# Input projections of a GRU scan moved between the start and the end of the scan

## The chip, the cores and the metric

The kernel runs on one NeuronCore of a Trainium2 chip. The metric is the device time of one execution in microseconds; the median of three runs of the kernel before is 1308.48 us (1308.43 to 1308.65). The core has a matrix engine (TensorE, PE), three engines for elementwise work (VectorE or DVE, ScalarE or ACT, GpSimd or POOL) and a queue engine (SyncE, SP) that only issues DMAs. Each engine executes its own list of instructions in order and waits on semaphores for the others.

## The reference

A GRU scans 256 time steps for 16 sequences of width 512. Its outputs pass through a mixture of eight low-rank experts, the best two per token, and the result is added to x. All data are float32.

```python
def cell(h, x):
    gi = x @ W_ih + b_ih            # 512 x 1536
    gh = h @ W_hh + b_hh            # 512 x 1536
    r = sigmoid(i_r + h_r)
    z = sigmoid(i_z + h_z)
    n = tanh(i_n + r * h_n)
    return (1 - z) * n + z * h

hs = scan(cell, cond, x over time)
logits = hs / norm(hs) @ router_w
top-2 of softmax(logits), renormalised -> combine
out = x + sum over e of combine[e] * (hs @ Wa[e] @ Wb[e])
```

gh of a step needs the step before; gi needs only x, and can be computed at any earlier moment.

## The kernel before, in words

**Layout.** 16 sequences fill only 16 rows of a matmul's stationary operand, so the kernel puts the four quarters of the 512 columns side by side on the array: every product is made in four column strips of 32, and a block of W (128 x 1536) is split along the contraction into four quarters q. A "pair" m is two consecutive time steps (2m and 2m+1) held together in 32 rows; there are 128 pairs, and four pairs (eight steps) make a block of x of which there are 32 (`NB`). The input side of a pair is `gate_in(m, q)` for q = 0 to 3 (L274): four matmuls of 256 columns for the gates r and n (L281), four of 128 columns for z (L289), accumulated in PSUM on top of a start value that ScalarE copies there, `seed(m)` (L255, L261). x must first be turned by VectorE, `trans_x(m)` (L266, L269).

**A step.** `step` (L903) multiplies the turned state with W_hh: r and n for all q (L914), then z (L924). ScalarE applies tanh for r (L940), for z (L945) and for n (L949); VectorE does the elementwise work between (L947 to L956) and turns the new state (L959) for the next step's matmuls, and back (L967). TensorE waits for L959 unless other matmuls fill the time. In the program, behind the recurrent matmuls of a step, stand half of `gate_in` for the next pair and then the pieces that a planner picks.

**The start.** SP issues, in this order: x of block 0 (`load_x`, L127: 8 DMAs of 32 KB), W_ih and W_hh (`load_w`, L152: 16 DMAs of 192 KB each, four per quarter q), x of block 1, the weights of router and experts (`wr_sb`, `wa_sb`, `wb_sb`, the last one DMA of 2 MB). `gate_in` for pair 0 and three quarters of pair 1 are computed as W_ih arrives. In step 0, `arrive(q)` scales a quarter of W_hh when it has come (L987 on VectorE, L988 on ScalarE), and behind it, for q = 1 to 3, eight matmuls of 512 columns on zeros (L993) are issued whose result nobody reads. The last quarter of pair 1 stands behind step 0's recurrent matmuls.

**The mixture.** 29 of the 32 blocks go a sparse way in four chunks of 7, 11, 7 and 4 blocks (`CHUNKS`). When a chunk is ranked, its tokens are scattered by expert (GpSimd, L551) into slots in DRAM; 86 slabs of 128 slots are then loaded (L652), multiplied by Wa (L691) and Wb (L706) and stored (L715), and gathered again for their tokens (`Combine`, L743, L757). A slab has four matmul pieces of 0.43 us by the planner's costs. Slabs of a chunk begin at the steps in `ready`: 73, 165, 217 and 246. The last three blocks are computed densely (`Moe`).

**The planner.** The whole order is written out when the program is built. Work besides the recurrence is cut into pieces with a cost on TensorE, a least distance in steps from the piece before (`gap`) and places that they take and give (`ROOM`). After each step `choose(spare)` picks pieces in order of rank: routes first, then slabs, combines, dense blocks and last the early pairs (rank 20). Pieces fit while their cost in this step is at most `spare`, which is 0.5, or 1.8 where the next pair needs no `gate_in` (`m + 1 in EARLY`); slabs and dense blocks have due times and can go beyond it on a credit that grows with how much is left.

**Early pairs.** For the pairs in `EARLY`, 82, 86, ... 126, twelve in all, the input side is computed in advance by an agent (`Early`, L359): load x of the pair (8 DMAs of 8 KB, L371), turn it (VectorE, L378), four pieces for r and n (L387), four for z (L392), `keep` (L397: ScalarE copies out of PSUM, GpSimd adds the bias), `store` to DRAM (L408), and `back` (L411, L413) loads it again from step 2m-16 on, for `seed(m)` to copy it into PSUM in place of the bias in step 2m-3. At most two agents work at once (`"early": 2`); they begin before step 2.

Of the kernel before, what the change touches and what calls it, by code (L numbers as in the profile page):

```python
# [8 lines left out]
FP = mybir.dt.float32  # L9
# [12 lines left out]
P = 128  # L22
# [3 lines left out]

EARLY = list(range(82, 128, 4))

# [16 lines left out]
def gru_moe_kernel(  # L45
# [11 lines left out]
    out: bass.AP,  # L57
):


# [33 lines left out]
    B, T, D = x.shape  # L94
    E, _, R = wa.shape
# [30 lines left out]

    def load_x(i):  # L127
        xt = xp.tile([P, NM, P], FP, tag="x", name=f"x_{i}")
        for j in range(NJ):
            for s in range(2):  # L130
                p0 = 32 * j + 16 * s
                sp.dma_start(
                    xt[p0 : p0 + B],
                    x[:, i * TS + s : (i + 1) * TS : 2, j * P : (j + 1) * P],
                )
        xs[i] = xt
# [23 lines left out]

    wih = load_w("wih", w_ih)
    whh = load_w("whh", w_hh)
    load_x(1)
# [91 lines left out]
    def seed(m):  # L255

        if m < T // 2:
            src = early.pop(m) if m in EARLY else bias
            for n, b in enumerate((src[:, 0:3, :], src[:, 3:4, :])):
                b = b.rearrange("p g d -> p (g d)")  # L260
                ins = act.copy(banks[m % 2][n][:, 0 : b.shape[1]], b).ins  # L261
                if seeds:
                    tc.add_manual_dep(ins, seeds[-1].name, SYNC, reason="seen")
                seeds.append(ins)

    def trans_x(m):  # L266
        if m < T // 2 and m not in EARLY:
            xt = xtp.tile([P, NQ, 32], FP, tag="xT", name=f"xT_{m}")
            dve.transpose(  # L269
                xt.rearrange("p q c -> p (q c)"), xs[m // NM][:, m % NM, :]  # L270
            )
            xts[m] = xt

    def gate_in(m, q, seen=None):  # L274

        if m in EARLY:
            return
# [81 lines left out]
    class Early:  # L359
# [5 lines left out]
        def load(self):  # L365
            m = self.m
            self.x = slb.tile([P, D], FP, tag="yg1", bufs=2, name=f"xe_{m}")
            for j in range(NJ):
                for s in range(2):
                    p0 = 32 * j + 16 * s  # L370
                    sp.dma_start(  # L371
                        self.x[p0 : p0 + B, 0:P],
                        x[:, 2 * m + s, j * P : (j + 1) * P],
                    )

        def turn(self):
            self.xt = slb.tile([P, NQ, 32], FP, tag="at", bufs=2, name=f"xTe_{self.m}")
            dve.transpose(self.xt.rearrange("p q c -> p (q c)"), self.x[:, 0:P])  # L378

# [17 lines left out]
        def keep(self):  # L397
            gi = slb.tile([P, 4, P], FP, tag="yg0", bufs=2, name=f"ge_{self.m}")
            act.copy(gi[:, 0, :], self.ps[:, 0, :])
            act.copy(gi[:, 2:4, :], self.ps[:, 2:4, :])  # L400
            pool.tensor_copy(gi[:, 1, :], bias[:, 1, :])
            pool.tensor_add(gi[:, 0, :], gi[:, 0, :], bias[:, 0, :])
            pool.tensor_add(gi[:, 2:4, :], gi[:, 2:4, :], bias[:, 2:4, :])
            self.gi = gi

        def store(self):
            self.dram = dramc.tile([P, 4, P], FP, name=f"gd_{self.m}")
            sp.dma_start(self.dram, self.gi)  # L408
            at_step(2 * self.m - 16, self.back)

# [4 lines left out]
        def plan(self):  # L415
# [8 lines left out]
            pieces[2].gap, pieces[2].takes = 1, ["ps"]  # L424
            pieces[9].then, pieces[9].gives = [("keep",)], ["ps", "at"]
            return pieces

# [551 lines left out]
    seed(1)  # L979
    for m, q in [(0, q) for q in range(NQ)] + [(1, q) for q in range(NQ - 1)]:  # L980
        gate_in(m, q)

    def arrive(q):


        cut = 2 * D
        dve.tensor_scalar_mul(whh[:, q, 0:cut], whh[:, q, 0:cut], 0.5)  # L987
        act.mul(whh[:, q, cut:G], whh[:, q, cut:G], 0.5)  # L988
        if q:
            idle = big(f"idle_{q}")  # L990
            for _ in range(2):
                for j in range(NJ):
                    pe.matmul(  # L993
                        idle[32 * j : 32 * j + 32, :], lhsT=zero[:, 0:32], rhs=zero,
                        start=True, stop=True,
                    )


# [7 lines left out]
    def at_step(n, make):  # L1006
        starts.setdefault(n, []).append(make)
# [98 lines left out]
    for i in range(NB):  # L1106
        rows, rows_next = rows_next, None
        for t in range(TS):
# [82 lines left out]
```

## Time and profile before

| | value |
|---|---|
| median of three runs | 1308.48 us (1308.43 to 1308.65) |
| the profiled execution, its own time | 1301.67 us |
| its span, first to last instruction | 1299.9 us |
| mean granted TensorE clock | 0.992 |
| W_hh's last quarter is scaled at | 35.8 us |
| step 1 begins at | 39.57 us |
| last turn of the state (L959) begins at | 1218.9 us |
| TensorE busy | 1252.2 us (96%) |

A line of the groups or of the timeline gives start and duration in us, engine, source line, operation, output tile, inputs, and in brackets how long the engine stood idle before and what ended that. Lines of waits give in total who waited for whom, how often, and the longest. A line of windows gives a stretch of time, then the busy time of PE, PEld (weight loads), DVE, ACT and POOL with their numbers of instructions, the granted share of TensorE's clock, the share of the 16 DMA engines that was busy, and GB/s.

### The profile page before, as it was taken

To read this page: it belongs to the slowest core of one execution; us is meant where nothing else is said; L and a number is where in the kernel's file an instruction comes from. 1 tells how busy PE (TensorE), PEld (TensorE's weight loads), DVE (VectorE), ACT (ScalarE), POOL (GpSimd) and SP (SyncE) were. 2 spreads that over 40 slices of the span, in tenths; PEclk is the share of its full clock that TensorE was granted. 3 is DMA by queue.
4 is the path that set the end of the run, shared out by engine and by line. 5 is a ranking of instruction groups with operands and counts; after the bars stand their busy time and mean duration, and the time that the engine had idled before them with its cause. 6 is when DMAs were issued, how large, how long until landed. Compare 5 with 4: busy or idle time off the path is not lost. (4 is left out here: it accounts for less than half of the span.)

```text
span 1299.9 us, 68450 instructions
## 1 busy us (share of the span) xinstructions
PE 1252.2 (96%) x30378; PEld 888.0 (68%) x30378; DVE 734.4 (56%) x2678; ACT 391.4 (30%) x1354; POOL 285.4 (22%) x504
## 2 busy tenths in 40 slices
PE   6799999999999999999999999999999999999996
PEld 2477777777777777777777766777777777777652
DVE  1445555555555555555556646666556556676643
ACT  1222232222223333233232323333333333333320
POOL 2000000000421100000100433232114234373552
PEclk7999999999999999999999999999999999999999
DMA  8522322321522221112111544655335446774786
GB/s 196 158 98 86 103 91 80 104 92 47 191 77 62 60 61 54 49 44 60 43 56 57 193 153 122 173 163 150 97 98 184 150 134 183 207 224 144 206 256 179
DMA packets 149477, 158.67 MB, mean 122 GB/s; under 512 B 22646, under 2 KB 103606, under 8 KB 149180
## 3 DMA queue, kind: packets, MB, share of 16 engines
q1 hardware_dynamic: 139760, 123.83, 32.2%
q0 software_dynamic: 9280, 30.42, 7.5%
q8 instruction: 238, 3.90, 1.3%
q14 instruction: 59, 0.48, 0.1%
q10 hardware_dynamic: 140, 0.05, 0.0%
HBM read 84.21 MB, written 69.99 MB: 119 GB/s over the span
## 5 line engine op out<-in xcount | busy, mean ns | idle before, releaser
L914 PE MATMUL rn<-whh,hist 128*32 128x256 f32 x8160 | 493.6, 382 | 19.4 <-DVE hist L959 16.5
L914 PEld LDWEIGHTS rn<-whh,hist 128*32 128x32 f32 x8160 | 247.7, 110 | 201.4 <-DVE hist L959 51.8
L281 PE MATMUL rn<-wih,xT 128*32 128x256 f32 x3712 | 287.9, 381 | 11.3 <-DMA wih<-in_L_cond_W_ih_dram 9.4
L947 DVE SCALAR_TENSOR_TENSOR n<-r,rn 128x128 f32<-128x128 f32 x256 | 73.2, 286 | 362.2 <-ACT r L940 361.2
L924 PE MATMUL z<-whh,hist 128*32 128x128 f32 x8160 | 271.0, 273 | 0.0
L924 PEld LDWEIGHTS z<-whh,hist 128*32 128x32 f32 x8160 | 235.5, 110 | 42.9 <-issue 0.4
L940 ACT ACTIVATE r<-rn 128x128 f32<-128x128 f32 x256 | 70.9, 277 | 426.4 <-PE rn L914 426.4
L289 PE MATMUL z<-wih,xT 128*32 128x128 f32 x3712 | 188.4, 274 | 0.0
L289 PEld LDWEIGHTS z<-wih,xT 128*32 128x32 f32 x3712 | 122.0, 111 | 80.4 <-issue 1.8
L281 PEld LDWEIGHTS rn<-wih,xT 128*32 128x32 f32 x3712 | 112.0, 110 | 12.9 <-DMA wih<-in_L_cond_W_ih_dram 5.1
L945 ACT ACTIVATE z<-z 128x128 f32<-128x128 f32 x256 | 71.0, 278 | 151.1 <-PE z L924 150.5
L952 DVE SCALAR_TENSOR_TENSOR zh<-z,h 128x128 f32<-128x128 f32 x255 | 77.7, 305 | 65.6 <-ACT z L945 65.4
L622 POOL TENSOR_TENSOR nrm<-ss,half 128x1 f32<-128x1 f32 x29 | 16.2, 560 | 411.5 <-ACT ht L620 392.4
L691 PE MATMUL at_ps<-xgT,wag 128*32 128x128 f32 x2752 | 96.8, 273 | 2.2 <-POOL nrm L808 1.4
L706 PE MATMUL y_ps<-wbg,at 128*32 128x256 f32 x1376 | 94.6, 380 | 0.8 <-ACT at L698 0.8
L691 PEld LDWEIGHTS at_ps<-xgT,wag 128*32 128x32 f32 x2752 | 79.1, 110 | 9.8 <-issue 3.1
L959 DVE STREAM_TRANSPOSE hist<-rows 128x128 f32<-128x128 f32 x256 | 79.8, 312 | 8.7
L967 DVE STREAM_TRANSPOSE h<-hist 128x128 f32<-128x128 f32 x256 | 79.7, 311 | 8.7
L956 DVE SCALAR_TENSOR_TENSOR rows<-zh,m 128x128 f32<-128x128 f32 x256 | 76.0, 297 | 8.9
L674 POOL COPY wbg<-wb_sb 128x512 f32 x86 | 55.4, 644 | 114.9 <-PE y_ps L706 114.9
L949 ACT ACTIVATE n<-n 128x128 f32<-128x128 f32 x256 | 77.3, 302 | 7.6 <-DVE n L948 7.3
L714 ACT COPY y<-y_ps 128x512 f32<-128x512 f32 x86 | 50.1, 583 | 94.9 <-PE y_ps L706 85.7
(136 smaller groups left out, 1050.4 us busy)
## 6 DMA issues: line engine op xcount, KB each, us to landing
xg<-x_slots SPq DMA_DIRECT2D x344, 64.0 KB
y_slots<-y SPq DMA_DIRECT2D x86, 256.0 KB
ht<-H SPq DMA_DIRECT2D x58, 256.0 KB
x_slots<-zero SPq DMA_DIRECT2D x50, 256.0 KB
x<-in_x_dram SPq DMA_DIRECT2D x256, 32.0 KB
xr<-in_x_dram SPq DMA_DIRECT2D x32, 256.0 KB
out_dram<-xr SPq DMA_DIRECT2D x32, 256.0 KB
H<-rows SPq DMA_DIRECT2D x232, 32.0 KB
```

What stands on the lines that cost most here:

```text
L281: pe.matmul(rn[32 * j : 32 * j + 32, 0 : 3 * P].rearrange("p (g d) -> p g d", g=3)[:, 0:3:2, :], lhsT=xts[m][:, q, :], rhs=w[:, 0:3:2, j, ...
L289: ins = pe.matmul(zb[32 * j : 32 * j + 32, 0:P], lhsT=xts[m][:, q, :], rhs=w[:, 1, j, :], start=False, stop=(q == NQ - 1), skip_group_chec ...
L691: pe.matmul(self.ps[c32, 0:P], lhsT=self.wa[:, q, c32], rhs=self.xt[:, q, :], start=(q == 0), stop=(q == NQ - 1),)
L706: pe.matmul(self.ps[c32, half], lhsT=self.at[:, c32], rhs=self.wb[:, half], start=True, stop=True,)
L914: pe.matmul(rn[32 * j : 32 * j + 32, 0 : 2 * P].rearrange("p (g d) -> p g d", g=2), lhsT=hT[:, q, :], rhs=w(q, j)[:, 0:3:2, :], start=Fals ...
L924: pe.matmul(zb[32 * j : 32 * j + 32, 0:P], lhsT=hT[:, q, :], rhs=w(q, j)[:, 1, :], start=False, stop=(q == NQ - 1), skip_group_check=True,)
L947: dve.scalar_tensor_tensor(n, r, 1.0, rn[:, P : 2 * P], ALU.add, ALU.mult)
L949: act.activation(n, n, AF.Tanh)
L952: dve.scalar_tensor_tensor(zh, z, 1.0, hrow, ALU.add, ALU.mult)
L956: dve.scalar_tensor_tensor(hn, zh, 0.5, m, ALU.mult, ALU.subtract)
L959: dve.transpose(hist[:, t, :, lo : lo + 32], hn.rearrange("p (q c) -> p q c", q=NQ))
L967: dve.transpose(hrow.rearrange("p (q c) -> p q c", q=NQ), hT)
```

## The change

- The input sides of pairs 2 and 3 (`HEAD`) are computed ahead of the scan by the methods of `Early`: pair 2 behind those of pairs 0 and 1, pair 3 in `arrive`, its r and n behind the first quarter of step 0 and its z behind the second. The results stay in SBUF. The last quarter of pair 1 moves ahead of step 0 as well. The matmuls on zeros go.
- x of block 21 (`EARLY[0] // NM`, pairs 84 to 87) is loaded between W_ih and W_hh and not again later.
- `EARLY` is 84 to 87 and then 92, 95, ... 125: sixteen pairs. The first four take x from that block, without loads, and turn in the step in which they begin; the others turn three steps after their load, before two.
- The agents begin before step 0, and `spare` is 1.8 in steps 0 and 1 and before a `HEAD` pair (steps 2 to 5) too.
- Early results are loaded again from step 2m-6 on.

```diff
-EARLY = list(range(82, 128, 4))
+EARLY = [84, 85, 86, 87] + list(range(92, 128, 3))
+HEAD = [2, 3]
...
-    def load_x(i):
-        xt = xp.tile([P, NM, P], FP, tag="x", name=f"x_{i}")
+    def load_x(i, pool=xp, tag="x"):
+        xt = pool.tile([P, NM, P], FP, tag=tag, name=f"x_{i}")
...
     wih = load_w("wih", w_ih)
+    load_x(EARLY[0] // NM, slb, "xg")
     whh = load_w("whh", w_hh)
...
-            src = early.pop(m) if m in EARLY else bias
+            src = early.pop(m) if m in EARLY + HEAD else bias
...
-        if m < T // 2 and m not in EARLY:
+        if m < T // 2 and m not in EARLY + HEAD:
...
-        if m in EARLY:
+        if m in EARLY + HEAD:
             return
...
         def load(self):
             m = self.m
+            if m in EARLY[:4]:
+                return
...
+            if m in HEAD + EARLY[:4]:
+                rows = xs[m // NM][:, m % NM, :]
+            else:
+                rows = self.x[:, 0:P]
+            dve.transpose(self.xt.rearrange("p q c -> p (q c)"), rows)
...
         def keep(self):
-            gi = slb.tile([P, 4, P], FP, tag="yg0", bufs=2, name=f"ge_{self.m}")
+            tag, bufs = ("xg", 4) if self.m in HEAD else ("yg0", 2)
+            gi = slb.tile([P, 4, P], FP, tag=tag, bufs=bufs, name=f"ge_{self.m}")
...
+            if self.m in HEAD:
+                early[self.m] = gi
...
-            at_step(2 * self.m - 16, self.back)
+            at_step(2 * self.m - 6, self.back)
...
+            pieces[1].gap = 0 if self.m in EARLY[:4] else 3
...
-    for m, q in [(0, q) for q in range(NQ)] + [(1, q) for q in range(NQ - 1)]:
-        gate_in(m, q)
+    for m in (0, 1):
+        for q in range(NQ):
+            gate_in(m, q)
+    head = [Early(m) for m in HEAD]
+    for agent in head:
+        agent.turn()
+    for what in ("rn", "z"):
+        for q in range(NQ):
+            head[0].into(what, q)
+    head[0].keep()
...
-        if q:
-            idle = big(f"idle_{q}")
-            for _ in range(2):
-                for j in range(NJ):
-                    pe.matmul(
-                        idle[32 * j : 32 * j + 32, :], lhsT=zero[:, 0:32], rhs=zero,
-                        start=True, stop=True,
-                    )
+        if q == 1:
+            for n in range(NQ):
+                head[1].into("rn", n)
+        elif q == 2:
+            for n in range(NQ):
+                head[1].into("z", n)
+            head[1].keep()
...
-    at_step(2, lambda: [begin(Early(m), 20) for m in EARLY])
+    at_step(0, lambda: [begin(Early(m), 20) for m in EARLY])
...
-            if m == 0:
-                if t == 0:
-                    gate_in(1, NQ - 1, seen)
-            elif m + 1 < T // 2:
+            if 0 < m and m + 1 < T // 2:
...
-            picked = choose(1.8 if m + 1 in EARLY else 0.5)
+            picked = choose(1.8 if m == 0 or m + 1 in EARLY + HEAD else 0.5)
...
-            if t == 3 and i + 2 < NB:
+            if t == 3 and i + 2 < NB and i + 2 not in xs:
                 load_x(i + 2)
```

More of the change, by code (lines that the diff above doesn't have):

```diff
@@ L376, in turn @@
         def turn(self):
-            self.xt = slb.tile([P, NQ, 32], FP, tag="at", bufs=2, name=f"xTe_{self.m}")
-            dve.transpose(self.xt.rearrange("p q c -> p (q c)"), self.x[:, 0:P])
+            m = self.m
+            self.xt = slb.tile([P, NQ, 32], FP, tag="at", bufs=2, name=f"xTe_{m}")
+            if m in HEAD + EARLY[:4]:
[3 more added lines that the diff above has]
+            dve.transpose(self.xt.rearrange("p q c -> p (q c)"), rows)
         def into(self, what, q):
```

## The prediction

> **What bounds the kernel now.** I read the engine shares first, then who waits for whom, then single steps in the timeline, then windows of the start.
>
> ```profile
> PE 1252.2 (96%) x30378; PEld 888.0 (68%) x30378; DVE 734.4 (56%) x2678; ACT 391.4 (30%) x1354; POOL 285.4 (22%) x504
> ...
> PE rn L914 <- DVE hist L959: 16.5, 25, 3.8
> ```
>
> TensorE looks full, but "busy" includes matmuls that only fill a wait. The timeline of single steps (step n counted from 0; it begins at the first L914 row) tells more:
>
> ```profile
> 52.78 1.93 PE L914 MATMUL rn<-whh,hist 128*32 128x256 f32 x32 [0.30 <-DVE hist L959]
> ...
> 57.19 1.93 PE L914 MATMUL rn<-whh,hist 128*32 128x256 f32 x32 [0.30 <-DVE hist L959]
> ...
> 102.44 1.93 PE L914 MATMUL rn<-whh,hist 128*32 128x256 f32 x32
> 104.19 1.06 PE L924 MATMUL z<-whh,hist 128*32 128x128 f32 x32
> 105.06 0.61 PE L281 MATMUL rn<-wih,xT 128*32 128x256 f32 x8
> ...
> 106.36 0.61 PE L387 MATMUL gi<-wih,xTe 128*32 128x256 f32 x8
> 106.85 1.93 PE L914 MATMUL rn<-whh,hist 128*32 128x256 f32 x32
> ```
>
> Step 4 (52.78) has no early work and takes 4.41 us; step 15 (102.44) has one early matmul group of 0.43 us more and takes 4.41 us too. So a step has a floor of 4.40 us, its chain of gates, and room for about 4.34 us of TensorE work: 2.62 recurrent (102.44 to 105.06), 1.30 for the input side of the next pair (105.06 to 106.36), 0.43 of anything else. What exceeds that is paid one for one:
>
> ```profile
> 1082.84 1.91 PE L914 MATMUL rn<-whh,hist 128*32 128x256 f32 x32
> ...
> 1086.73 1.06 PE L691 MATMUL at_ps<-xgT,wag 128*32 128x128 f32 x32
> 1087.61 1.91 PE L914 MATMUL rn<-whh,hist 128*32 128x256 f32 x32
> ```
>
> Here 0.87 us of slab work makes the step 4.77. Listing all step starts, time above 4.405 per step is 5.6 us in steps 1 to 7, 0.7 in 8 to 77, 6.2 in 78 to 161, 22.8 in 162 to 221 and 21.2 from 222 on; after the last step (1218.9) TensorE works off what is left until 1290. So work taken out of late steps is worth its full time, work put into early free room costs nothing.
>
> **What steps 5 and 6 lose.** They begin at 57.19 and 65.51, and step 7 at 71.60: 14.41 us where 8.81 would do.
>
> ```profile
> 63.12 0.31 DVE L378 STREAM_TRANSPOSE xTe<-xe 128x128 f32<-128x128 f32 x1 [4.58 <-DMA xe<-in_x_dram]
> ...
> 65.51 3.02 PE L914 MATMUL rn<-whh,hist 128*32 128x256 f32 x32 [3.78 <-DVE hist L959]
> ```
>
> The transposition of the second early pair's x waits on VectorE, in order, ahead of the gates of step 5; its loads were issued behind the 2 MB of W_b. The pause also halves TensorE's clock (L914 takes 3.02 instead of 1.93).
>
> **The parts, one by one.**
>
> *1. That stall goes: -5.6 us.* The first four early pairs (84 to 87) read block 21 of x, which is there before W_hh. The first pair with loads of its own (92) gets a place only when the third is stored, in step 9, some 30 us after W_b is in, and turns three steps later. If the stall only moves, 0; its whole amount is the other bound.
>
> *2. x of block 21 ahead of W_hh: +2.5 us.* Eight more DMAs on SP move W_hh (16), x of block 1 (8) and the other weights (21) back. 256 KB at the 230 GB/s of the neighbouring windows would be 1.1 us. But the same kind of load after W_hh leaves a hole:
>
> ```profile
> 32.00:33.00 1.00, 0.62 (x8) 0.00 (x0) 0.26 (x1) 0.28 (x1) 0.00 (x0) 1.00 1.09 250
> 33.00:34.00 1.00, 0.46 (x10) 0.37 (x13) 0.43 (x1) 0.35 (x1) 0.00 (x0) 1.00 0.87 163
> 34.00:35.00 1.00, 1.00 (x20) 0.50 (x16) 0.00 (x0) 0.00 (x0) 0.00 (x0) 1.00 0.45 87
> ...
> 37.00:38.00 1.00, 1.00 (x28) 0.52 (x20) 0.40 (x2) 0.50 (x2) 0.00 (x0) 1.00 0.27 60
> 38.00:39.00 1.00, 0.23 (x8) 0.00 (x0) 0.79 (x4) 0.31 (x1) 0.00 (x0) 1.00 0.85 245
> ```
>
> The last column is GB/s. In the trace each SP DMA waits for the semaphore of the one eight before it, so while eight small ones are in flight no large one is queued. The first DMA behind block 1 of x is issued 0.30 us after the last quarter of W_hh is used (36.06 against 35.76). So W_hh's first issue comes at 22.33 (last quarter of W_ih used) + 0.3 = 22.6; W_ih itself took 5.6 us from first issue (5.23) to first use (10.83); hence W_hh's first quarter at 28.2 instead of 25.82: 2.4, taken as 2.5. Bounds 1.1 and 3.5. All of it is on the path: step 0 ends with the last quarter. The other weights that move back have long slack (W_a and W_b are first read in step 77, block 1 of x in step 4).
>
> *3. Pairs 2 and 3 in the head: 0 on the path.* Each is 16 matmuls of each kind, 2.6 us. Pair 1's last part and pair 2 follow the seven groups that now end at 26.6, so TensorE is free at about 29.8. ScalarE's copies of pair 2 (0.27 + 0.38 us) stand ahead of its scaling of W_hh's first quarter, so that scaling slips from 28.3 to 30.4. Pair 3's parts (1.72 and 0.87) go where the filler matmuls were (3 x 1.72, removed) and its copies stand before the last scaling. The last quarter arrives at 35.76 + 2.5 = 38.3; everything ahead of it on TensorE is done near 36.6. The cover is thus about 1.7 us; without it, what exceeds it is paid. GpSimd's three operations per pair (0.29 + 0.46 + 0.73) are read by seeds at the ends of steps 1 and 3. VectorE's two transpositions lie in the wait.
>
> *4. The clock: +2.0 us.* Without filler matmuls TensorE now pauses from 36.6 to 39.0, works 0.65, and pauses again for the gates of step 0 (2.3 us, formerly cut by pair 1's last part).
>
> ```profile
> 10.00:15.00 5.00, 1.61 (x24) 0.96 (x28) 0.00 (x0) 1.27 (x4) 0.00 (x0) 0.66 1.03 225
> 15.00:20.00 5.00, 1.80 (x25) 0.91 (x20) 0.00 (x0) 0.00 (x0) 0.00 (x0) 0.50 1.02 226
> ```
>
> PEclk (last but two) is 0.66 in the first window: full for 1.6 us, half from about 11.6 on. Before that drop stood a pause of only 1.7 us, 0.9 of work and the start of a pause of 2.6. [...] Half clock adds 0.65 to the last quarter's matmuls and about half of the 2.7 us until it recovers inside step 1. Step 6 paid 6.08 - 4.41 = 1.67 for the same. Bounds 0 and 3.
>
> *5. Early work in steps 1 to 5: 0 now, worth it later.* By the planner's rules step 1 takes 1.72 us of pair 84, steps 2 and 3 take 1.74 each, step 4 none (the next pair must turn first), step 5 takes 1.72, then 0.43 to 0.44 a step. Work of 2.62 + 1.74 fits the floor. Pair 87 ends in step 14, so four pairs are done where one and a half were. At the old pace of 6.7 steps a pair, 13 to 14 are done when slabs take the room (step 78), against 11. The other two or three find room in steps 166 to 169, free of input work while the slabs of the second chunk, which start at 165 and need five steps, aren't ready.
>
> *6. 16 late pairs instead of 12: -7.8 us.* Every early pair frees 1.30 us in two steps, and the planner puts up to 1.8 us of slabs there. From step 170 on, where load exceeds room, there were 22 such steps and are now 28: 6 x 1.30. In steps 170 to 222 the second chunk needs 29 x 1.72 = 50 us, and even the new room is some 43, so none should be idle. Bounds: -3.9 (half unused) and -10.4 (four pairs in full).
>
> *7. The reload.* Pairs are read back from step 2m-6 instead of 2m-16, with the seed (ScalarE) in step 2m-3: three steps and 3.2 us, about 16.5 us. Reloads in the trace are issued up to 12.8 us after their step begins (step 212, behind scatters and x) and land 2.3 to 4.8 us later. The worst is at the edge; mostly 5 us remain. Behind a late seed stand tanh and all later gates. 0, with +4 as bound.
>
> *8. Contention.* Two or three late pairs share buffers with the first combines; steps 169 and 172, where one did so, were 0.5 long each. +0.5, bounds 0 and 3.
>
> Sum: -5.6 + 2.5 + 2.0 - 7.8 + 0.5 = -8.4 us against the profiled execution's 1301.67 (span 1299.9 and 1.8 around it), so 1293.3 there. The runs' median lies 6.8 higher; the same difference gives 1308.48 - 8.4 = **1300.1 us**.
>
> **Rivals.**
>
> *Better:* the clock stays up and the load costs its bytes only: -2.0 and -1.4, so 1296.7. [...]
>
> *The freed steps stay half empty*, because slabs aren't loaded in time for eight free steps in a row: 3.9 less, and 1 more of contention, 1305.0. For it: steps 220 and 221 have no slab today; against: the room still falls short of the need.
>
> *The stall only moves:* 5.6 less, 1305.7. Against it: steps 8 to 77 show no such wait.
>
> *Slower: the late reload.* In the seed (L261), if issue plus landing passes 16.5 us. The four pairs whose reload falls behind an x load (85, 101, 113, 125) at 4 us each give 1316. It decides from 8.4 us in total, half a microsecond per pair. For it: three steps instead of thirteen, in the part with 143 to 225 GB/s; against: the landings above.
>
> **How the numbers follow.** Forecast 0.52, better 0.14, half empty 0.14, stall moves 0.05, late reload 0.15. A measurement tells 0.2% (2.6 us) from nothing. Half empty and stall moved lie near that edge (1305.9): 0.10 of their 0.19 counts as faster, the rest as the same; of the late reload 0.01 is the same and 0.14 slower. Faster 0.76, same 0.10, slower 0.14. The likeliest's own range is 1297.5 to 1303.5; with the other cases and the bounds it is 1295.5 to 1308.0, leaving out the reload and a little below.
>
> **What would show it.** Right: steps 5 and 6 at 4.4; W_hh's scalings 2 to 3 us later; half clock near 39 us; step 7 within 1.5 us of 71.6; steps 166 to 173 at 4.4 to 4.5. Wrong: ScalarE waiting for gl; the last quarter's matmuls behind pair 3; a new VectorE wait for xe; steps above 5 us after 170 as before.

## The result

The changed kernel takes 1313.32 us (median of 22 runs, 1307.61 to 1319.53) where the kernel before takes 1308.43 (22 runs beside it, 1304.80 to 1310.59): ratio 1.0052, 95% interval 1.0041 to 1.0063. It is slower by 4.9 us in the medians and by 6.8 (5.4 to 8.2) by the ratio, which is what I use from here on; the forecast was 8 us faster, and its range ended at 1308.0. The profiled execution of the changed kernel took 1310.03 us (span 1308.3, clock 0.988) against 1301.67 (1299.9, 0.992).

One profiled execution lies up to some 4 us on either side of its kernel's median (b_norm3's 6.0 above), and the profile of before lies 6.8 below. So in what follows a stage of a profile counts where several kernels show the same, and prices are taken from the ratios.

**The start went as forecast.** From the timeline of the changed kernel (start, duration, engine, line, operation):

```profile
38.42 0.69 DVE L1010 TENSOR_SCALAR whh<-whh 128x1024 f32<-128x1024 f32 x1 [2.07 <-DMA x<-in_x_dram]
39.22 1.08 PE L930 MATMUL rn<-whh,h0T 128*32 128x256 f32 x8 [1.91 <-DMA x<-in_x_dram]
42.76 3.47 PE L930 MATMUL rn<-whh,hist 128*32 128x256 f32 x32 [2.03 <-DVE hist L975]
...
62.38 1.93 PE L930 MATMUL rn<-whh,hist 128*32 128x256 f32 x32 [1.68 <-DVE hist L975]
62.51 0.27 DVE L390 STREAM_TRANSPOSE xTe<-x 128x128 f32<-128x128 f32 x1
66.78 1.93 PE L930 MATMUL rn<-whh,hist 128*32 128x256 f32 x32
71.19 1.07 PE L930 MATMUL rn<-whh,hist 128*32 128x256 f32 x16
```

The last quarter of W_hh is scaled at 38.42 (35.76 before), its matmuls and those of step 1 run at half clock (1.08 and 3.47 us), steps 5 and 6 take 4.40 and 4.41 us with no wait for xTe, and step 7 begins at 71.19 (71.60 before). Yet the wait that the forecast meant to shrink grew. Who waits for whom, in the changed kernel (us in total, times, longest):

```profile
PE rn L930 <- DVE hist L975: 22.4, 29, 2.0
...
ACT ht L636 <- DMA ht<-H: 15.2, 5, 5.5
ACT y L730 <- DMA y_slots<-y: 14.3, 6, 5.2
```

It was 16.5 us with a longest of 3.8: the one long wait is gone, and many of about one microsecond have come.

**Where the time came from.** I split each step: TensorE's busy time above 4.405 us is called load, and what the step took beyond the larger of 4.405 and that busy time is called wait. Differences to the kernel before, in us, from the profiled executions (b_16, below, has the new list of late pairs and the old start):

| stage | forecast | after | b_16 |
|---|---|---|---|
| up to step 8 | -1.1 | -0.4 | -1.1 |
| steps 8 to 77 | 0 | +2.3 | +0.1 |
| steps 78 to 161 | 0 | +3.1 | +5.1 |
| steps 162 to 169 | +0.5 | +0.2 | -1.8 |
| steps 170 to 254 | -7.8 | -1.1 | -1.2 |
| behind the start of the last step | 0 | +4.3 | +5.9 |
| sum | -8.4 | +8.4 | +7.0 |

In steps 170 to 254 the load fell from 36.3 to 27.9 us, by 8.4, as the forecast had it (7.8). But the wait rose from 3.7 to 11.0. Here is one such step in the timeline, step 182, which begins at 862.82 and lasts 5.18 us. Before, it took 5.42, with 0.58 of load and 0.44 of wait; now it has no load and 0.77 of wait:

```profile
862.82 1.91 PE L930 MATMUL rn<-whh,hist 128*32 128x256 f32 x32
...
864.87 0.61 POOL L686 COPY wag<-wa_sb 128x512 f32 x1 [0.55 <-PE rn L930]
865.11 0.29 DVE L963 SCALAR_TENSOR_TENSOR n<-r,rn 128x128 f32<-128x128 f32 x1 [0.21 <-ACT r L956]
...
865.43 0.29 DVE L964 SCALAR_TENSOR_TENSOR n<-n,rn 128x128 f32<-128x128 f32 x1
865.43 0.60 POOL L690 COPY wbg<-wb_sb 128x512 f32 x1
...
866.12 0.63 POOL L686 COPY wag<-wa_sb 128x512 f32 x1
866.19 0.70 DVE L970 SCALAR_TENSOR_TENSOR m<-z,n 128x128 f32<-128x128 f32 x1
...
866.70 0.67 POOL L690 COPY wbg<-wb_sb 128x512 f32 x1
866.92 0.58 DVE L972 SCALAR_TENSOR_TENSOR rows<-zh,m 128x128 f32<-128x128 f32 x1
...
868.00 0.42 PE L930 MATMUL rn<-whh,hist 128*32 128x256 f32 x4 [1.09 <-DVE hist L975]
```

GpSimd copies a slab's weights (L686, L690) while VectorE does the gates. L970 takes 0.70 us and ends 0.14 after the copy that it met; L972 takes 0.58 and ends 0.13 after the next one. The medians of their 256 are 0.28 and 0.29. TensorE, with less to do than before, stands idle for 1.09 us behind them. In this step VectorE's list shows no wait for GpSimd: the lost time is inside the duration of L970 and L972. It is so in most late steps: of the changed kernel's wait behind step 170, 9.7 of some 11 us stand in the 14 steps in which the gate operations together took at least 0.25 us more than 0.29 apiece.

### The profile page after: what moved, and what is told of

Same layout as the page of the kernel before. It is cut to its first block, busy times and chain, and to the rows that moved or that the text cites. A ratio compares the mean times of both kernels' runs of the same rounds, so it can differ in the third digit from the quotient of the medians.

```text
span 1308.3 us, 68408 instructions
## 1 busy us (share of the span) xinstructions
PE 1247.6 (95%) x30330; PEld 891.8 (68%) x30330; DVE 741.3 (57%) x2678; ACT 394.5 (30%) x1366; POOL 292.5 (22%) x522
## 4 chain that ended last, share of the span: by engine, by line
PE 82%; DMA 6%; DVE 5%; issue 2%; ACT 1%; SPq 1%; POOL 1%; POOLq 0%; ACTq 0%; DVEq 0%
PE rn L930 33%; PE z L940 16%; PE rn L286 12%; PE z L294 6%; PE y_ps L722 4%; PE at_ps L707 4%; PE gi L399 2%; DMA ht<-H 1%; PE a_ps L842 1%; DVE m L970 1%; DVE rows L972 1%; DMA wih<-in_L_cond_W_ih_dram 1%; PE rt L358 1%; PE gi L404 1%; DMA whh<-in_L_cond_W_hh_dram 1%
## 5 line engine op out<-in xcount | busy, mean ns | idle before, releaser
L930 PEld LDWEIGHTS rn<-whh,hist 128*32 128x32 f32 x8160 | 251.5, 110 | 205.9 <-DVE hist L975 50.1
L286 PE MATMUL rn<-wih,xT 128*32 128x256 f32 x3520 | 274.1, 382 | 12.5 <-DMA wih<-in_L_cond_W_ih_dram 9.0
L963 DVE SCALAR_TENSOR_TENSOR n<-r,rn 128x128 f32<-128x128 f32 x256 | 73.6, 287 | 363.6 <-ACT r L956 361.2
L956 ACT ACTIVATE r<-rn 128x128 f32<-128x128 f32 x256 | 70.9, 277 | 422.0 <-PE rn L930 422.0
L294 PE MATMUL z<-wih,xT 128*32 128x128 f32 x3520 | 179.7, 274 | 0.0
L294 PEld LDWEIGHTS z<-wih,xT 128*32 128x32 f32 x3520 | 117.4, 111 | 75.0 <-issue 2.0
L286 PEld LDWEIGHTS rn<-wih,xT 128*32 128x32 f32 x3520 | 107.2, 111 | 14.3 <-DMA wih<-in_L_cond_W_ih_dram 4.6
L968 DVE SCALAR_TENSOR_TENSOR zh<-z,h 128x128 f32<-128x128 f32 x255 | 79.2, 311 | 65.5 <-ACT z L961 64.9
L972 DVE SCALAR_TENSOR_TENSOR rows<-zh,m 128x128 f32<-128x128 f32 x256 | 78.3, 306 | 8.9
L970 DVE SCALAR_TENSOR_TENSOR m<-z,n 128x128 f32<-128x128 f32 x256 | 78.8, 308 | 1.5 <-ACT n L965 1.2
L690 POOL COPY wbg<-wb_sb 128x512 f32 x86 | 54.8, 637 | 109.8 <-PE y_ps L722 109.8
L964 DVE SCALAR_TENSOR_TENSOR n<-n,rn 128x128 f32<-128x128 f32 x256 | 73.6, 287 | 8.8
```

The source lines that it names most:

```text
L286: pe.matmul(rn[32 * j : 32 * j + 32, 0 : 3 * P].rearrange("p (g d) -> p g d", g=3)[:, 0:3:2, :], lhsT=xts[m][:, q, :], rhs=w[:, 0:3:2, j, ...
L294: ins = pe.matmul(zb[32 * j : 32 * j + 32, 0:P], lhsT=xts[m][:, q, :], rhs=w[:, 1, j, :], start=False, stop=(q == NQ - 1), skip_group_chec ...
L930: pe.matmul(rn[32 * j : 32 * j + 32, 0 : 2 * P].rearrange("p (g d) -> p g d", g=2), lhsT=hT[:, q, :], rhs=w(q, j)[:, 0:3:2, :], start=Fals ...
L963: dve.scalar_tensor_tensor(n, r, 1.0, rn[:, P : 2 * P], ALU.add, ALU.mult)
L968: dve.scalar_tensor_tensor(zh, z, 1.0, hrow, ALU.add, ALU.mult)
L970: dve.scalar_tensor_tensor(m, z, 1.0, n, ALU.subtract, ALU.mult)
```

## The experiments

All ratios are to runs of the kernel before on the same chip (its medians there were 1306.6 to 1309.5), with 95% intervals; a difference between two of them is uncertain by some 2 to 3 us. Every name that begins with a_ is the changed kernel with an edit, b_ the kernel before with one.

### Copies of the weights left out: a_nocopy, b_nocopy

```diff
-            e = pool.value_load(self.chunk.expert[0:1, n : n + 1], ...)
-            self.wa = slb.tile([P, NQ, R], FP, tag="wag", ...)
...
-            pool.tensor_copy(self.wa, wa_sb[:, :, bass.ds(e, 1), :]...)
-            pool.tensor_copy(self.wb, wb_sb[:, bass.ds(e, 1), :]...)
+            self.wa = wa_sb[:, :, 0, :]
+            self.wb = wb_sb[:, 0, :]
```

These two leave out the choice of the expert: all slabs use the weights of expert 0.

> The changed kernel without GpSimd's copies of a slab's expert weights; every slab multiplies with expert 0's weights where they lie, so the output is not the reference's. Theory (GpSimd slows VectorE): the elementwise operations of the gates that took 0.58 to 0.73 us instead of 0.29 beside these copies go back to 0.29; the time lost to stalls in steps 170 to 255, 11.0 us against 3.7 in the kernel before, falls to about 4, and the kernel gets 6 to 9 us faster than with them. Rival (slabs' loads or PSUM set the freed steps): stalls stay at 9 or more.

> The kernel before with the same left out: slabs use expert 0's weights in place, without copies. Theory (GpSimd slows VectorE): this kernel gains less than the changed one, 1 to 3 us, because its late steps are bound by TensorE and cover the slower gates; so without copies the changed kernel is no longer slower than it by 7 but within 2 of it. Rival: both gain the same and the difference of about 7 us stays.

Measured: a_nocopy 1303.30 us, ratio 0.9971 (0.9955 to 0.9988); b_nocopy 1300.85, 0.9952 (0.9938 to 0.9966). The edit takes some 10.5 us from the changed kernel and 6.3 from the old one, and the gap between the two falls from 6.8 us to 2.5. The copies cost both kernels time, and account for about 4 us of the difference; by the intervals that can be 1 to 7.5. Neither side of the expectations holds whole: the gains are larger than was said for both kernels (6 to 9 and 1 to 3), and the wait from step 170 on is 7.2 us, between the 4 of the theory and the 9 of the rival. Of these 7.2, 4.9 are step 214 alone, where VectorE stands behind GpSimd (5.23 us idle before L329), and GpSimd behind a fetch of ht. The edit also spares TensorE any wait for the copied weights, but such waits of its weight loads come to only 2.6 us in the changed kernel and 1.3 in the old one.

### Copies in quarters: a_split, b_split

```diff
-            pool.tensor_copy(self.wa, wa_sb[:, :, bass.ds(e, 1), :]...)
+            for q in range(NQ):
+                pool.tensor_copy(self.wa[:, q, :], wa_sb[:, q, bass.ds(e, 1), :]...)
...  # the same for wb
```

> The kernel after, with each of GpSimd's two copies of a slab's weights (128x512) written as four of 128x128; the same bytes are copied. Theory 1, a gate operation of VectorE that meets a copy waits until that copy has ended (in the trace of the changed kernel 14 of the slow gate operations end 0.14 to 0.16 us after a copy's end, whenever they began): a wait is then at most one quarter's length, so the excess of the gate operations over 0.29 us, 15.2 us in all in the changed kernel, falls below 8, and the time by 2 to 6 us, to 1307 to 1311. Theory 2, the two engines share a rate while both run: the excess depends on how long copies run, and stays at 13 us or more, the time within 1.5 us of the changed kernel's 1313.3, or longer by the three more starts per copy. Theory 3, the copies matter because weights come late to TensorE: pieces that end no sooner change nothing, within 1.5 us.

> The kernel before with the same quarters. Theory 1: its excess of 10.3 us falls below 6, but most of it lay in steps whose end TensorE's work set; the time falls by 1 to 4 us, less than that of the kernel after. Theories 2 and 3: within 1.5 us of the kernel before.

Measured: a_split 1316.35, ratio 1.0056 (1.0033 to 1.0079); b_split 1304.78, 0.9976 (0.9961 to 0.9990). In the profiles the gate operations' excess over 0.29 us fell from 15.2 to 11.3 us in the changed kernel and from 10.3 to 8.1 in the old. Both fell less than theory 1 had it (below 8 and below 6) and more than theory 2 (13 or more in the changed kernel), so the excess doesn't decide between them. The old kernel's gain is as expected; for the changed one the forecast of 2 to 6 us failed. Its profile shows waits of 1 to 3 us in steps 164, 169, 188, 208 and 214 and lost clock behind three of them; why quarters helped one kernel and not the other stays open.

### Copies by DMA: a_spdma, b_spdma

```diff
-            e = pool.value_load(
+            e = sp.value_load(
...
-            pool.tensor_copy(self.wa, ...)
-            pool.tensor_copy(self.wb, ...)
+            sp.dma_start(self.wa, ...)
+            sp.dma_start(self.wb, ...)
```

> The kernel after with the two copies of each slab's weights taken off GpSimd: SyncE reads the expert's number and issues two transfers from the weights in SBUF to the slab's buffers. The result is unchanged. Theory, GpSimd's copies held VectorE's gate operations: their excess over 0.29 us, 15.2 us in all, falls below 7, the stalls from step 170 on from 11.0 us to 6 or less, and the time comes near that of the kernel with the copies left out (1303.3): 1303 to 1307. Rival, SyncE's queue is the scarcer one: 58 more transfers of some 0.5 us each to issue, and waits for the expert's number and for free buffers in it, so the loads behind them come late and ACT and VectorE wait for transfers: over 1310, with stalls before DMA-fed instructions in place of slow gate operations.

> The same edit on the kernel before. By the theory about 6 us less than before, as the kernel without copies: 1301 to 1304, and so 2 to 3 us below the edited kernel after, where the two unedited kernels are 5 us apart. By the rival 1308 or more.

Measured: a_spdma 1379.69 us, ratio 1.0529 (1.0488 to 1.0571); b_spdma 1371.06, 1.0464 (1.0425 to 1.0503). Both theories are right in their own half. (The 58 transfers of the expectation are those of one chunk; all slabs have 172.) VectorE's five gate operations, from the groups of the changed kernel (busy time, mean ns of one, idle before):

```profile
L963 DVE SCALAR_TENSOR_TENSOR n<-r,rn 128x128 f32<-128x128 f32 x256 | 73.6, 287 | 363.6 <-ACT r L956 361.2 <-issue 2.0
L968 DVE SCALAR_TENSOR_TENSOR zh<-z,h 128x128 f32<-128x128 f32 x255 | 79.2, 311 | 65.5 <-ACT z L961 64.9 <-issue 0.5
L972 DVE SCALAR_TENSOR_TENSOR rows<-zh,m 128x128 f32<-128x128 f32 x256 | 78.3, 306 | 8.9
L970 DVE SCALAR_TENSOR_TENSOR m<-z,n 128x128 f32<-128x128 f32 x256 | 78.8, 308 | 1.5 <-ACT n L965 1.2
L964 DVE SCALAR_TENSOR_TENSOR n<-n,rn 128x128 f32<-128x128 f32 x256 | 73.6, 287 | 8.8
```

and the same groups of a_spdma:

```profile
L968 DVE SCALAR_TENSOR_TENSOR zh<-z,h 128x128 f32<-128x128 f32 x255 | 74.9, 294 | 61.9 <-ACT z L961 61.7
L972 DVE SCALAR_TENSOR_TENSOR rows<-zh,m 128x128 f32<-128x128 f32 x256 | 74.9, 292 | 8.9
...
L970 DVE SCALAR_TENSOR_TENSOR m<-z,n 128x128 f32<-128x128 f32 x256 | 73.6, 287 | 4.1 <-ACT n L965 3.8
L964 DVE SCALAR_TENSOR_TENSOR n<-n,rn 128x128 f32<-128x128 f32 x256 | 73.6, 287 | 8.7
```

L968, L970 and L972 are back at 287 to 294 ns, and their excess is 2.4 us in all where it was 15.2: GpSimd's copies held them. But the transfers cost more than that. Waits of a_spdma:

```profile
ACT y L730 <- DMA y_slots<-y: 48.0, 13, 8.4
ACT ht L636 <- DMA ht<-H: 46.8, 11, 7.2
```

They were 14.3 and 15.2 us above. In steps 170 to 254 the wait is 37.6 us, against 11.0. Whether SyncE's issuing or the 45 MB more in the DMA engines (205.9 in all, 160.8 before the edit) is the scarcer, these runs don't tell.

### Fewer late pairs with the new start: a_14, a_12, a_14_split

```diff
-EARLY = [84, 85, 86, 87] + list(range(92, 128, 3))
+EARLY = [84, 85, 86, 87] + list(range(92, 122, 3))     # a_14
+EARLY = [84, 85, 86, 87] + list(range(93, 125, 4))     # a_12
```

> The changed kernel with 14 early pairs, without 122 and 125. Theory (early work past step 78 is paid for, and the steps it frees later are partly lost): overflow in steps 78 to 161 falls from 8.1 back to about 5 us, late steps lose 5.2 us of room but only about half of it in time; about 1 us faster than the changed kernel. Rival (each pair is worth its 2.6 us, the step of the prediction): 5.2 us less room, about 2 us slower than the changed kernel.

> The kernel after with 12 late pairs (84 to 87 and eight more, one in four, up to 121) where it has 16; the head, the x of block 21 ahead of W_hh and the late load of the stored sums stay. Theory, all of the loss lies in the four more pairs (computed beside slabs in steps 78 to 161, and taken from late steps that the gates then bound): the time is that of before within 2 us, 1307 to 1310, and near that of 14 pairs. Rival, the loss lies in what 12 pairs keep (the changed start, the late loads): 1311 to 1314. A third, the two pairs from 14 to 12 were worth their 2.6 us each: 1312 to 1314 as well, but with 5 us more overflow from step 170 on and no more stall.

> The kernel after with 14 late pairs and with GpSimd's copies in quarters. If quarters shorten the holds as in the old kernel (by 3 us there), 1304 to 1307 where 14 pairs alone gave 1308.4. If what the quarters give is lost again to their eight starts per slab and to the wait for weights that come later, 1308 to 1312.

Measured: a_14 1308.42 us, ratio 1.0009 (0.9992 to 1.0025); a_12 1311.15, 1.0026 (1.0013 to 1.0039); a_14_split 1310.54, 1.0026 (1.0006 to 1.0046). Two pairs fewer are worth 5.6 us, more than the 1 us that was expected; the next two are worth nothing or cost a little. The profiles show why: from a_14 to a_12 the load of steps 170 to 254 rises from 30.5 to 35.3 us, and the wait falls from 10.2 to 5.3, so work put back there costs next to nothing. But a_12 missed its first expectation (the time of before within 2 us): with as many pairs as the old kernel it is 3.4 us slower, as its rival had it, so the number of pairs is not the whole loss. The stage that differs in its profile is the one behind the start of the last step, 7.5 us longer. In a_14 the load of steps 78 to 161 is 3.4 us (8.1 with 16 pairs, 4.5 before). Quarters on top of 14 pairs bring nothing.

### The new list alone, the late reload alone, fewer pairs: b_16, b_late, b_10, b_7

```diff
-EARLY = list(range(82, 128, 4))
+EARLY = [84, 85, 86, 87] + list(range(92, 128, 3))     # b_16
+EARLY = list(range(90, 128, 4))                        # b_10
+EARLY = list(range(102, 128, 4))                       # b_7
...
-            at_step(2 * self.m - 16, self.back)
+            at_step(2 * self.m - 6, self.back)             # b_16 and b_late
```

> The kernel before with the list of 16 late pairs and the reload at step 2m-6, and nothing of the new head: x of block 21 not ahead of W_hh, pairs 2 and 3 as before, early pairs from step 2. If the longer list carries the loss, it is slower than before by 4 us or more, 1312 to 1317, with the early pairs' work in steps 78 to 161 (overflow above 6 us there, 4.5 before) and more slow gate operations from step 170 on. If the new head carries it, the list keeps a gain of its own: 1303 to 1307.

> The kernel before with the reload of a stored pair issued at step 2m-6 in place of 2m-16, and nothing else. If the reload is hidden, as the forecast had it, the time is within 1.5 us of before (1307 to 1310). If it lands in SyncE's queue where later transfers or ACT's wait stand behind it, 1311 or more, with stalls after step 162 that the old kernel does not show.

> The kernel before with 10 late pairs (90 to 126 in fours) in place of 12. By the forecast's price of a late pair (2.6 us, two freed steps of 1.30) it is 5 us slower, 1313. If a step that a pair frees is mostly bound by its gates, and the pairs dropped are those computed beside slabs after step 78, the time is within 2 us of before, 1306 to 1310.

> The kernel before with 7 late pairs (102 to 126 in fours). With 10 all early work already lies before step 78, in room that nothing else uses, so three pairs fewer save nothing early and put six full steps more behind step 170 (2 x 1.30 us each by the trace's late steps): if a late pair whose early work is free is worth its 2.6 us, 8 us slower than 10 pairs, 1311 to 1314. If TensorE's excess in such a step is mostly replaced by the wait for the gates, within 3 us of 10 pairs, 1304 to 1308.

Measured: b_16 1312.48 us, ratio 1.0047 (1.0030 to 1.0064); b_late 1305.77, 0.9992 (0.9977 to 1.0008); b_10 1304.85, 0.9985 (0.9970 to 0.9999); b_7 1311.33, 1.0023 (1.0009 to 1.0037).

b_16 is as slow as the whole change, without any of its new start. So the new list carries the loss, by its length, its places or its end, and b_late clears the reload. Where the early work of the pairs went is read from windows of the tile gi (the early matmuls), first before, then after, then b_16. Each window is about steps 78 to 161; the first number behind its length is PE's busy time in it, with the number of matmul records:

```profile
385.00:761.00 376.00, 1.99 (x44) 1.15 (x40) 0.52 (x2) 1.00 0.24 71
```

```profile
387.00:766.00 379.00, 7.44 (x132) 3.74 (x128) 1.62 (x6) 1.00 0.23 70
```

```profile
384.00:765.00 381.00, 16.77 (x300) 8.64 (x296) 2.68 (x10) 1.00 0.24 71
```

The load of this stage is 4.5, 8.1 and 10.9 us in these three. At 2.6 us for a pair's 64 matmuls, the 88 more of the changed kernel are 3.6 us of work and raise the load by 3.6: paid in full, beside slabs that already fill the room. The 256 more of b_16 are 10.4 us and raise it by 6.4: six tenths. b_10 has none of it there, nor have a_12 and a_14.

From b_7 to b_10 three pairs are worth 5.0 us (0.0038 of 1308), 1.7 each; their load from step 170 on differs by 7.3 us, 2.4 each, near the forecast's 2.6. From 10 to 12 pairs the ratio rises from 0.9985 to 1, with the interval just short of 1. From 12 to 16 (b_16) the four pairs cost 1.5 us each, if all of b_16's loss is put on them; its list also differs in places and end. The forecast's price is near for the first three and has the wrong sign for the last four.

### The stall of steps 5 and 6 alone, and filler matmuls: b_begin8, a_fill

```diff
-    at_step(2, lambda: [begin(Early(m), 20) for m in EARLY])
+    at_step(8, lambda: [begin(Early(m), 20) for m in EARLY])       # b_begin8
```

```diff
+    def filler(name):                                              # a_fill
+        idle = big(name)
+        for _ in range(2):
+            for j in range(NJ):
+                pe.matmul(idle[32 * j : 32 * j + 32, :], lhsT=zero[:, 0:32], rhs=zero, ...)
...  # called in arrive(3), and behind the recurrent matmuls of step 0
```

> The kernel before with one number changed: the early pairs begin at step 8 and not at step 2, so that the transfer of their x no longer stands behind W_hh; nothing is loaded ahead of W_hh and no pair is computed beside its arrival. If the stall of steps 5 and 6 (3.8 us beside 1.7 us of slow clock behind it) is all that the head of the change had to gain, the time falls by 5.6 us less the price of work that comes six steps later: about one and a half pairs more after step 78, at 0.8 to 2.6 us each, so 2 to 4 us are left, 1304 to 1306 where the kernel before shows 1308. If such a stall only moves to the next late transfer, or the later pairs cost all of it, the time is within 1 us of before, or longer.

> The changed kernel with two filler blocks of eight matmuls on zeros put back where its start pauses: ahead of the last quarter's recurrent matmuls and behind them in step 0. Theory (the clock at the start): the changed kernel's 22 runs spread over 12 us (1307.6 to 1319.5) while their mean granted clock goes from 0.990 down to 0.984, so its half-clock time differs from run to run; with the fillers the clock stays full from 25 us on, step 2 begins about 2 us earlier than at 48.70, the median falls by 3 to 5 us to about 1309, and the spread shrinks to that of the kernel before. Rival (the loss is all behind step 8): the profile's start improves by at most 2 us and the median by no more.

Measured: b_begin8 1308.72 us, ratio 0.9996 (0.9977 to 1.0014); a_fill 1311.71, 1.0038 (1.0023 to 1.0052). In b_begin8 step 8 begins at 69.2 us instead of 76.0, and by step 78 only 1.0 us of that is left: step 71 waits 3.3 us for another x (VectorE 5.10 us idle before its transposition of xe) and step 72 runs at half clock. So here a stall that was removed did move, to a later transfer behind the same queue. a_fill keeps the clock at full through step 1 (step 8 begins at 73.6 instead of 75.6), and only 1.8 us come of it by the ratios, as the rival had it; the spread stays (11.5 us). In its profile the gain is lost like that of b_begin8: step 70 waits 3.4 us, and step 78 begins only 0.3 us earlier.

### The stalls of steps 68 and 164: a_norm3, b_norm3

The timeline of the changed kernel shows step 68, 6.04 us long:

```profile
337.90 0.32 SPq L621 DMA_DIRECT2D ht<-H  x1
...
338.27 4.61 SPq L378 DMA_DIRECT2D xe<-in_x_dram  x8
...
342.63 0.63 ACT L636 ACTIVATE ht<-ht 128x512 f32<-128x512 f32 x1 [3.45 <-DMA ht<-H]
...
343.97 0.27 ACT L956 ACTIVATE r<-rn 128x128 f32<-128x128 f32 x1
```

ACT's gate function L956 stands behind a norm (L636) that waits for a fetch, issued beside eight loads of x for an early pair.

```diff
-LAG = 10
+LAG = 11
...
-                Piece(gap=7, cost=0.9, pe=[("ranks",)],
+                Piece(gap=8, cost=0.9, pe=[("ranks",)],
...
-                Piece(gap=2, then=[("norm",)]),
+                Piece(gap=3, then=[("norm",)]),
```

> The kernel after with one step more between the fetch of a block's hidden states and ACT's norm over them, and the rest of the routing one step later (three numbers: 2 to 3, 7 to 8, 10 to 11). It tests the stalls of steps 68 and 164, where ACT's next gate function stands behind a norm that waits for the fetch: if the late fetch behind SyncE's queue is the cause, both stalls (1.3 and 3.3 us) shrink below 0.5 us each and the time falls by 2 to 5 us, to 1308 to 1311. If the stall is carried along (the fetch is released by something that moves with it), both stay and the time is within 1.5 us of 1313.3.

> The same three numbers in the kernel before, which has the stall at step 164 (2.5 us in its trace, 5.6 to 5.8 in three of its variants, with a half clock after it) and none at step 68: 2 to 5 us less than before, 1303 to 1306, if the late fetch is the cause; within 1.5 us of before if the stall is carried along.

Measured: a_norm3 1315.69 us, ratio 1.0047 (1.0029 to 1.0064); b_norm3 1316.94, 1.0065 (1.0044 to 1.0085). Both expectations failed in part: the waits of steps 68 and 164 are gone from both profiles (each below 0.25 us), and the time isn't shorter. In a_norm3 waits of 0.4 to 0.5 us stand in eight steps between 78 and 161, in b_norm3 one of 4.4 us in step 159. With every later piece of the plan one step off, this is no clean test of what these two stalls are worth.

### The two helpful edits together: b_split_10

The list of b_10 and the quarters of b_split.

> The kernel before with 10 late pairs and GpSimd's copies in quarters. Each edit alone gave 1.7 and 3.3 us. If they act on different stages (the pairs on steps 78 to 170, the quarters on VectorE's gate operations) they add to about 5 us, 1301 to 1303; if not, 1303 to 1306.

Measured: 1305.23 us where the kernel before takes 1309.53, ratio 0.9968 (0.9955 to 0.9980). Expected were 1301 to 1303 beside a kernel before of 1308 if the edits add, 1303 to 1306 if not; scaled by its ratio it is 1304.2. But the two single gains (0.15 and 0.24%) sum to 0.39%, and the interval of the measured 0.32% reaches from 0.20 to 0.45: whether they add isn't decided. It leaves nothing out and is faster than both kernels, by 0.3% and 0.8%.

## Why the prediction was wrong

**Parts 1 to 4, the start: right.** The stall of steps 5 and 6 is gone (wait 3.8 to 0.25 us in steps 1 to 7). The last quarter came 2.65 us later (2.5 forecast). The clock: 0.44 us in the last quarter's matmuls and 1.53 in step 1, 1.97 together (2.0). Half clock came as part 4's row had it; the 2.7 us until it ends inside step 1 were an estimate of mine that no row was given for, and the changed kernel's trace has 3.17 (42.76 to 45.93). The whole start was to give 1.1 us and gave 0.4. The value of part 1 by itself was less sure than the sum let it look: with the same stall removed in another way (b_begin8) it came back 66 steps later.

**Part 5, early work that is free: half right.** Before step 78, 13 of the 16 late pairs were done (832 matmul records of gi behind the start of step 1, 64 to a pair), within the forecast's 13 to 14. But "the other two or three find room in steps 166 to 169" failed: one did. Two were computed in steps 78 to 161 beside slabs, where the stage grew by 3.1 us, while steps 168 and 169 kept 2.7 us of room unused. b_16 shows it larger (4.6 pairs, 5.1 us) and a_14, with the same start and two pairs fewer, shows the stage 1.5 us below the old kernel's. The planner gives an early pair its place by rank and room in the present step; it doesn't keep it for a better one. I had read the room as if it did.

**Part 6, the sum's large term: the load was right, its worth wrong.** The step that failed is "what exceeds that is paid one for one ... so work taken out of late steps is worth its full time". The load fell by 8.4 us and the steps by 1.1. The gap between forecast and profile is 16.8 us, and 6.7 of it lie here. One for one held where TensorE ended last in the step, as in the step of 4.77 us at 1082.84. The floor of 4.405 us was read from steps 4 and 15, where GpSimd copies no weights. In late steps the chain of gates is longer by whatever the copies hold (0.41 and 0.29 us in step 182), which the extra TensorE work used to cover: the gate operations' excess in steps 170 to 254 was 5.0 us before and 10.9 after. The rows were in the groups of before too, where zh, m and rows take longer on average than the two n; I didn't compare them:

```profile
L952 DVE SCALAR_TENSOR_TENSOR zh<-z,h 128x128 f32<-128x128 f32 x255 | 77.7, 305 | 65.6 <-ACT z L945 65.4 <-issue 0.3
L954 DVE SCALAR_TENSOR_TENSOR m<-z,n 128x128 f32<-128x128 f32 x256 | 77.5, 303 | 1.5 <-ACT n L949 1.4
L956 DVE SCALAR_TENSOR_TENSOR rows<-zh,m 128x128 f32<-128x128 f32 x256 | 76.0, 297 | 8.9
L948 DVE SCALAR_TENSOR_TENSOR n<-n,rn 128x128 f32<-128x128 f32 x256 | 73.5, 287 | 8.8
L947 DVE SCALAR_TENSOR_TENSOR n<-r,rn 128x128 f32<-128x128 f32 x256 | 73.2, 286 | 362.2 <-ACT r L940 361.2 <-issue 0.8
```

That the copies hold the gates is shown by a_spdma. How much of the gap between the two kernels they make is less sure: the copy-free pair puts it at 4 of 6.8 us, with 1 to 7.5 within the intervals.

Which operations are held shows in the trace. In the changed kernel an operation L963 or L964, which takes one input from PSUM, overlapped a copy of weights 55 times, and none took over 0.29 us; L968, L970 or L972, with two inputs in SBUF, did so 59 times, and 38 took over 0.40. Of the 39 gate operations that took over 0.45 us, 38 ended 0.10 to 0.18 us after the end of a GpSimd instruction. By what means GpSimd holds them, no run shows. The trace of before has the same: of 56 operations L947 or L948 that overlapped a copy none took over 0.29 us, of 38 operations L952, L954 or L956 27 took over 0.40. It could be read there ahead of the forecast; how far it would have lowered the worth of part 6 was not shown.

**A term that the sum did not have:** behind the start of the last step the kernel takes 4.3 us longer. It shows in all the kernels with a new list that leave routing and SyncE's queue alone (the changed kernel, a_fill, a_nocopy, a_split, a_14, a_12, a_14_split, b_16): 89 to 93 us, where the eight whose list ends with pair 126 (before, b_nocopy, b_split, b_begin8, b_late, b_10, b_7, b_split_10) have 83 to 86. Part of it is the end, after the changed kernel's last matmul at 1296.1:

```profile
1293.37 0.54 SPq L806 DMA_DIRECT2D xr<-in_x_dram  x1
...
1300.22 0.69 DVE L889 TENSOR_TENSOR xr<-o_ps,xr 128x512 f32<-128x512 f32 x1 [9.72 <-DMA xr<-in_x_dram]
```

and before, after its last at 1289.8:

```profile
1288.17 0.54 SPq L790 DMA_DIRECT2D xr<-in_x_dram  x1
...
1292.53 0.69 DVE L873 TENSOR_TENSOR xr<-o_ps,xr 128x512 f32<-128x512 f32 x1 [1.69 <-DMA xr<-in_x_dram]
```

VectorE's addition of the last block begins 6.8 us after the issue of the load that it waits for, instead of 4.4. Why the rest of the tail is longer isn't settled: the new lists end at pair 125, 121 or 119, so the last steps free less room, but a list that differs in this alone was not run. What the profiles show: of the 4.3 us, TensorE's work behind the start of the last step is 0.7, its pauses there 1.5, and the time after its last matmul 2.0; seven of the eight kernels with a new list leave 240 matmuls of Wb for this stage and a_12 leaves 224, where the eight others leave 208. As a_12 shows the longer tail with only twelve pairs, the length of the list isn't what makes it; what does stays open.

**Part 7, the reload: right.** b_late's interval includes no change, and ACT has no wait for gl in the profile. **Part 8, contention:** what there was lay elsewhere: 2.3 us in steps 8 to 77 (steps 68 and 71), where the 16 pairs' transfers still share SyncE's queue with the first routes. In b_16 this stage lost nothing, so it goes with the new start.

**The rivals.** None was it. "Half empty" had the right place and the wrong mechanism: the late steps had work (steps 170 to 254 leave 4.4 us of TensorE's room unused, 4.8 before), and waited for VectorE. The rival on the slower side took a mechanism that the trace made unlikely, and left out the one whose rows stood in the groups.

**The clock** is a smaller part. In the 22 runs of the changed kernel the mean granted clock is 0.9868 and the time falls by 1.5 us for each 0.001; 55 runs of the old kernel on another chip have 0.9885 and 1.1 us. At these slopes the difference goes with 2 to 3 us. But a_fill, beside those same 55 runs, has 0.9894 and is still 0.38% slower, so the clock alone is not the cause.

## What to carry to other kernels

Work taken off the busiest engine is worth its time only down to the next bound of the same stage (here 8.4 us of load gave 1.1), so read that bound in that stage: compare the mean duration of equal operations on the other engine with and without neighbours, since here the hold lay inside durations (0.70 us for 0.29 in step 182) and the list of waits didn't show it. Moving work forward had a price at the place where it landed (3.1 us in steps 78 to 161), and here the last entries of the list got the worst places; change the length of such a list in both directions and measure, before adding to it. The forecast's price per entry (2.6 us) was not far off for entries 8 to 10 (1.7) and, as far as b_16 tells, had the wrong sign for 13 to 16.

## What the hardware showed that was not expected

- VectorE's gate operations of 0.29 us took up to 0.77 us, once 1.11, when GpSimd's copies of 128x512 (0.60 to 0.67 us in step 182) ran beside them in the changed kernel, and only those with both inputs in SBUF: the two with an input in PSUM took at most 0.29 in 55 overlaps.
- Ahead of the kernel's end, TensorE's half clock (0.50 granted) lasted 13.65 us from 11.6 on and 3.41 from 66.2 on in the kernel before, and 13.65 from 11.8 on and 6.83 from 39.1 on in the changed one. The length of a wait alone didn't tell here whether half clock followed: behind waits of 3.1 to 5.6 us in step 5, step 6 took 5.70 to 7.10 us in eight kernels, with half clock, and 4.40 in b_late and b_nocopy, at full clock after waits of 3.4 and 3.7.
- SyncE took 4.61 us to issue eight loads of x of 8 KB each beside step 68 of the changed kernel. With 172 transfers more (two for each of the 86 slabs) the two kernels that copy by DMA are 4.6% and 5.3% longer, and in the changed one ACT's waits for y_slots and ht grow from 29.5 to 94.8 us.
